# A bias network's third layer: tiles of 16 keys with two lane sums, or tiles of 32 keys with a third lane sum by transfers

## The chip, the cores and the metric

One Trainium2 chip, one core. The metric is the device time of one execution in microseconds. The kernel before was run three times: 2618.71, 2620.34 and 2621.09 us, median 2620.34. One further execution was taken by the hardware profiler.

## The reference, cut to what matters

The module has two layers: a deformable attention with an MLP behind it, and a plain attention. The change is in the first layer's attention. It has 16 groups (batch 2 times 8 heads), each with 1024 queries (32 x 32 pixels) and 64 keys at positions that the network itself has computed. For every pair of a query and a key, a small network of three layers turns the difference of their positions into one number, which is added to the product of query and key:

```python
pos = grid_q[:, :, None, :] - grid_kv[:, None, :, :]      # 2 numbers for each pair
bias = jnp.sign(pos) * jnp.log1p(jnp.abs(pos))
bias = jax.nn.relu(bias @ cpb_w1 + cpb_b1)                # 2 -> 128   (layer 1)
bias = jax.nn.relu(bias @ cpb_w2 + cpb_b2)                # 128 -> 128 (layer 2)
bias = (bias @ cpb_w3 + cpb_b3)                           # 128 -> 1   (layer 3)
sim = jnp.einsum('bhid,bhjd->bhij', qh, kh) + bias
attn = jax.nn.softmax(sim, axis=-1)
```

That is 16 x 1024 x 64, about a million pairs, and layer 2 alone is a product of 128 x 128 for each. This bias network is most of the kernel's time.

## The kernel before, in words

**Stages.** Some 35 us of head (first queries, offsets, weights); then one loop over 256 slices, from about 35 to 1892 us; then the output projection, the MLP and the second attention layer. The change touches the loop, and a little of the head that prepares weights and the order of channels.

**A slice** is four keys of one group against all 1024 queries; a group is 16 slices (NSL), and s counts the slices through. In one slice:
- `st_layer1` (L681, DVE): one custom instruction adds two tables, ta (x part) and tb (y part), and clips below at zero, into h (three buffers). It is made two slices ahead.
- `st_layer2` (L698, TensorE): 32 matmuls of 128 x 32 weights. For each z of four sets of 32 channels, four column groups of the array take the four keys, so that partition 32 q + l of the PSUM tile holds key q and lane l. Each z is evicted by ACT with its relu (L707 for z = 0 and 2 into rx; L709 for z = 1 and 3, with a scale).
- `st_sum` (L717, DVE): one scalar_tensor_tensor adds z = 0 to z = 1, another adds z = 2 to z = 3, with layer 3's weights as the scale. The first sum is in a tile called ua, uo or uc by the slice (s % 4 = 0: ua; odd: uo; 2: uc); the second is in ub. Then a DMA issued by POOL adds ub onto the first (L719). Layer 3 is now the sum over 32 lanes, with one sign for each.

**Lane sums by transfers.** The 32 lanes of a key are not summed on TensorE alone. Transfers that accumulate (issued by POOL, L736) and plain copies (issued by SP) fold the lanes and put two slices into one tile:
- `st_fold` adds odd lanes onto even lanes (64 partitions); `st_join` copies the next slice's odd lanes into the free odd lanes on SP (L743), and adds its even lanes there. A tile now has 8 keys by 16 lane sums.
- `st_fold2` and `st_join2` do the same with lanes in twos, on two slices further (32 partitions each, two of each; SP copies at L752). A tile ua now has 16 keys by 8 lane sums.

All adds go out on POOL in one fixed order, since `add` and `st_sum` chain them:

```python
        def add(out, in_):
            with tc.issue_after(added[0]):
                nc.gpsimd.dma_start(out=out, in_=in_, accum_op=ALU.add)
            added[0] = nc.cur_bb.bb.instructions[-1]
```

**Layer 3** (`st_layer3`, L784, TensorE) multiplies such tiles by a mask of signs (w3f) and accumulates into the PSUM tile sim, which also gets the product of query and key (L767, once for two groups). It is called at s % 8 = 4 for the 8 slices that began 12 slices before: two tiles, and for each of the two halves of the queries, four matmuls in the four column groups. For the last 8 slices of all, the slices that aren't folded to the end are multiplied one by one with w3u.

**What runs beside.** `softmax_steps` (tails) takes sim of a finished group in small steps, one per slice at most, on ACT, DVE and TensorE (transposes L801 and L834). `later` (bg) samples keys and makes the next chains' offsets in small steps. `load_tables` loads fb on SP one chunk of four slices ahead. The order of each engine's instructions is fixed when the program is built: a scheduler places them by priority, and `issue_after` forces some places. Iteration s means what the loop issues for s: the sums of slice s - 1, the folds and joins that are due, layer 1 of s + 2, layer 2 of s, and then layer 3.

**Buffers.** rx 3, ub 3, uo 3, uc 2, ua 4, h 3, PSUM tiles of layer 2 three. The rank and order of the channels in the head (`rank`, `order`, `arrange`) sorts them by the sign of their weight in layer 3, so that lanes which are added without a scale carry one sign.

Of the kernel before, what the change touches and what calls it, by code (L numbers as in the profile page):

```python
# [14 lines left out]
P = 128  # L15
# [4 lines left out]
J = 64  # L20
# [37 lines left out]
def conv_seq_kernel(ctx: ExitStack, tc: tile.TileContext, x, xt, kst, pst, cst, vec, wsm, outw, w1, w2, wl, wlt, brow, out):  # L58
# [24 lines left out]
    sc = cp.tile([P, 9], F32, name="sc")  # L83
    w3f = cp.tile([P, 48], F32, name="w3f")
    w3u = cp.tile([P, 60], F32, name="w3u")
# [121 lines left out]
    with tc.tile_pool(name="lp", bufs=2) as lp:  # L207
# [33 lines left out]
        nc.gpsimd.dma_start(out=cs, in_=cst)  # L241
        nc.gpsimd.dma_start(out=pz[:, 0:413], in_=pst)
        nc.gpsimd.dma_start(out=ident, in_=kst)

        def load(b, k, wq=None):
# [25 lines left out]
        po_, rn, t8, pc, dc, k8, one = (  # L271
            pw_[:, a:b] for a, b in ((0, 1), (1, 3), (3, 4), (4, 5), (5, 6), (8, 16), (128, 256))
        )
# [14 lines left out]
        def order():  # L288
            nc.vector.tensor_scalar(k8, eight, rn[:, 1:2], 8.0, ALU.is_le, ALU.mult)
            nc.vector.tensor_reduce(t8, k8, AX.X, ALU.add)  # L290
            free, bound = ([t.rearrange("p (a b l) -> p b a l", a=2, b=2)[:, i] for t in (place, crow)] for i in (0, 1))
            nc.vector.tensor_scalar(bound[0], bound[1], t8, 64.0, ALU.is_ge, ALU.mult)
            nc.vector.tensor_tensor(bound[0], bound[0], bound[1], ALU.add)
            nc.vector.tensor_scalar(free[0], free[1], t8, None, ALU.add)
            nc.vector.tensor_scalar(perm, place, pc, None, ALU.is_equal)

        def arrange():
# [16 lines left out]
            for z in (1, 3):  # L314
                nc.gpsimd.tensor_tensor(sc[:, 4 + z : 5 + z], sc[:, 4 + z : 5 + z], sc[:, z : z + 1], ALU.mult)
            nc.gpsimd.tensor_scalar(w3f[:, 16:32], mask[:, 0:16], sc[:, 8:9], None, ALU.mult)
            nc.gpsimd.tensor_scalar(w3u[:, 28:32], mask[:, 16:20], sc[:, 8:9], None, ALU.mult)

# [3 lines left out]
        def chain(ci):  # L322
# [126 lines left out]

            fe = ph.tile([P, 5, n], F32, tag="fe", name="fe")  # L450
            pos, ab, u, ln, er = (fe[0:64, i, :] for i in range(5))
            nc.vector.tensor_scalar(pos, thf[0:64, 2 * n : 3 * n], -1.0, gq[0:64], ALU.mult, ALU.add)
            if ci > 0:
# [6 lines left out]

            nc.vector.scalar_tensor_tensor(er, u, 1.0, ab, ALU.subtract, ALU.subtract)
            rc = acc.rearrange("p a k y x -> p (a k y x)")[0:64, 0:n]
            nc.vector.reciprocal(rc, u)
            nc.vector.tensor_tensor(er, er, rc, ALU.mult)
            nc.vector.tensor_scalar(pos, pos, 0.0, 2.0, ALU.is_ge, ALU.mult)
            yield
            nc.vector.tensor_tensor(ln, ln, er, ALU.subtract)
            nc.vector.scalar_tensor_tensor(ab, pos, 1.0, ln, ALU.subtract, ALU.mult)
# [9 lines left out]
        def sample(ci):  # L478
# [9 lines left out]

            sg = ph.tile([P, 5, 2, K * J], F32, tag="fe", name="sg")
            hat = sg[:, 0:4].rearrange("p a f j -> p (a f j)")[:, 0 : 4 * K * J]  # L490
# [4 lines left out]
            nc.vector.tensor_tensor(sg[:, 4], sg[:, 0], sg[:, 1], ALU.mult)  # L495
            hx = ph.tile([P, 2, K, J], F32, tag="hx", name="hx")
            hxf = hx.rearrange("p f k j -> p (f k j)")
# [4 lines left out]
            for i, (b, k) in enumerate(G):  # L502
# [13 lines left out]

                kv, uv = (ph.tile([P, J], F32, name=name) for name in ("kv", "uv"))
                rowwise, natural = "p (e i t) -> p e i t", "p (i e t) -> p e i t"
                for f in range(2):
                    r, v = slice(64 * f, 64 * f + 64), sg[:, 4, f, i * J : (i + 1) * J]  # L520
                    nc.scalar.activation(
                        uv[r].rearrange(rowwise, e=2, t=16), v[r].rearrange(natural, e=2, t=16), AF.Copy,
                        scale=col("bn1b", k)[r],
                    )
                yield
# [5 lines left out]
                for t in range(8):  # L531
                    for f in range(2):
# [3 lines left out]
                        )  # L536
                nc.scalar.activation(
                    kv.rearrange(rowwise, e=2, t=16), ps[:, 0:J].rearrange(natural, e=2, t=16), AF.Copy,
                    scale=bns[:, k : k + 1],
                )  # L540
                nc.vector.tensor_tensor(kv, kv, uv, ALU.add)
# [149 lines left out]
        def st_layer2(s):  # L691
            h1 = h1s.pop(s)
            r = []
            for z in range(4):
                ps = zp.tile([P, 2, 512], F32, name="ps2")
                for h in range(2):
                    for q in range(4):
                        nc.tensor.matmul(  # L698
                            ps[32 * q : 32 * q + 32, h, :], cw2[:, 32 * z : 32 * z + 32],
                            h1[:, 16 * h : 16 * h + 16, q, :], start=True, stop=True,  # L700
                        )
                name, bufs = (
                    ("rx", 3), (("ua", 4), ("uo", 3), ("uc", 2), ("uo", 3))[s % 4], ("rx", 3), ("ub", 3)
                )[z]
                o = lp.tile([P, 2, 512], F32, name=name, bufs=bufs)
                if z % 2 == 0:
                    nc.scalar.activation(o, ps, AF.Relu, bias=sc[:, 4 + z : 5 + z])  # L707
                else:
                    nc.scalar.activation(o, ps, AF.Relu, bias=sc[:, 4 + z : 5 + z], scale=sc[:, z : z + 1])  # L709
# [45 lines left out]


        def st_layer3(s):
            gi, i = divmod(s // 8, NSL // 8)
            b, k, f = groups[gi]
            if gi not in sims:  # L760
                sims[gi] = simp.tile([P, 512], F32, name="sim")
            if f == 0 and i == 1:

                assert state[chain_of[b, k][0]] is None
                sims[gi + 1] = simp.tile([P, 512], F32, name="sim")
                for f_, h_, o, h in QUADS:
                    nc.tensor.matmul(  # L767
                        sims[gi + o][h_, :], kz[f_, b * NCH + k, :], qa[f_, b, k, h * 512 : (h + 1) * 512],
                        start=(o == 1), stop=False,
                    )  # L770
            w = w3f[:, 16 - 16 * i : 48 - 16 * i]
            parts = [[(w, sums[s + 4 * e][1])] for e in range(2)]
            if s + 8 == NS:

                w = [w3u[:, 28 - 16 * i - 4 * o : 60 - 16 * i - 4 * o] for o in range(4)]
                parts[1] = [(w[o], sums[s + 4 + o][1]) for o in range(4)]
                parts[1].append((w[3], sums[s + 7][3]))
                parts[0] = 4 * [None] + parts[0]
            for m in range(len(parts[1])):
                for h in range(2):  # L780
                    for e in range(2):
                        if parts[e][m]:
                            q, (w_, t) = 64 * h + 32 * e, parts[e][m]
                            nc.tensor.matmul(  # L784
                                sims[gi][q : q + 32, :], w_, t[:, h, :], start=(i == 0 and f == 0),
                                stop=(i == 1 and m == len(parts[e]) - 1),
                            )
            for o in range(8):
                sums.pop(s + o)
# [57 lines left out]
        for s in range(NS):  # L847
# [602 lines left out]
def _order(np):  # L1450
# [3 lines left out]

    place = np.where(z % 2 == 1, 8 * (l // 4) + l % 4 + 4 * (z // 2), 32 * (z // 2) + l)
    crow = np.broadcast_to(place, (P, P))
    tri = d[:, None] < d[None, :]
    eight = np.broadcast_to(8 * np.arange(1, 9), (P, 8))
    four = (4 * (d % 4) + d // 32)[:, None] == np.arange(16)
    alone = (d // 32)[:, None] == np.arange(4)  # L1460
    return np.concatenate([crow, tri, eight, d[:, None], four, alone], axis=1).astype(np.float32)

# [87 lines left out]
```

## Time and profile before

| what | value |
|---|---|
| median of 3 runs | 2620.34 us |
| profiled execution | 2621.32 us, span 2619.2 us |
| TensorE clock granted | 1.00 |
| busy in the span: PE, DVE, ACT, POOL | 2603.2, 2313.1, 1750.3, 815.7 us |
| layer 2 on TensorE (L698) | 16384 records, 1776.0 us busy |
| layer 3 on TensorE (L784, w3f) | 252 records, 35.0 us busy |
| DMA over the span | 407.74 MB, mean 156 GB/s |

How to read it: the span runs from the first to the last instruction; the execution's own time is 2.1 us longer. A line Lnnn is the line of the kernel's source. The names of tiles are printed without numbers (h1 is h, ps2 is ps, cw2 is cw). One fp32 matmul leaves two records. "Idle before" is the time that the engine stood before an instruction of the group, and the name behind the arrow is what ended it. POOL's and SP's rows are issues: the transfer itself lands some us later.

### The profile page before, as it was taken

To read this page: it belongs to the slowest core of one execution; us is meant where nothing else is said; L and a number is where in the kernel's file an instruction comes from. 1 tells how busy PE (TensorE), PEld (TensorE's weight loads), DVE (VectorE), ACT (ScalarE), POOL (GpSimd) and SP (SyncE) were. 2 spreads that over 40 slices of the span, in tenths; PEclk is the share of its full clock that TensorE was granted. 3 is DMA by queue.
4 is the path that set the end of the run, shared out by engine and by line. 5 is a ranking of instruction groups with operands and counts; after the bars stand their busy time and mean duration, and the time that the engine had idled before them with its cause. 6 is when DMAs were issued, how large, how long until landed. Compare 5 with 4: busy or idle time off the path is not lost.

```text
span 2619.2 us, 48156 instructions
## 1 busy us (share of the span) xinstructions
PE 2603.2 (99%) x19752; PEld 1019.5 (39%) x19752; DVE 2313.1 (88%) x1463; ACT 1750.3 (67%) x2325; POOL 815.7 (31%) x909
## 2 busy tenths in 40 slices
PE   9999999999999999999999999999999999999999
PEld 3333322333233232333333333334355665646556
DVE  7999999999999999999999999999776587666656
ACT  5887898878888887887887777777733242314041
POOL 1333333333333333333333333333332334200100
PEclk9999999999999999999999999999999999999999
DMA  5788877888887888787887888788787768400202
GB/s 188 176 174 185 190 171 168 182 182 195 169 178 171 180 171 200 173 179 166 185 182 165 180 177 177 167 185 177 151 211 169 150 143 172 91 17 1 73 0 57
DMA packets 167531, 407.74 MB, mean 156 GB/s; under 512 B 24944, under 2 KB 73216, under 8 KB 164624
## 3 DMA queue, kind: packets, MB, share of 16 engines
q0 software_dynamic: 100736, 259.43, 54.6%
q1 hardware_dynamic: 66144, 144.93, 15.8%
q8 instruction: 156, 2.56, 0.4%
q14 instruction: 63, 0.52, 0.1%
q10 hardware_dynamic: 432, 0.31, 0.0%
HBM read 82.15 MB, written 6.55 MB: 34 GB/s over the span
## 4 chain that ended last, share of the span: by engine, by line
PE 93%; DVE 3%; ACT 2%; issue 1%; DMA 0%; DVEq 0%; ACTq 0%
PE ps L698 64%; PE sw L1041 7%; PE sw L1200 7%; PE sw L160 6%; PE sw L988 2%; PE sw L1298 2%; PE sim L784 1%; PE psg L600 1%; DVE hm L137 1%; ACT rx L707 1%; PE psx L1276 1%; PE pkv L534 0%; PE sim L767 0%; PE pt L801 0%; PE pb L834 0%
## 5 line engine op out<-in xcount | busy, mean ns | idle before, releaser
L698 PE MATMUL ps<-h,cw 128*32 128x512 f32 x16384 | 1776.0, 592 | 6.1 <-ACT rx L707 5.0
L681 DVE CUSTOM_DVE_ANT_1 h<-ta,tb 128x4096 f32<-128x4096 f32 (+1 forms) x257 | 1130.5, 4399 | 29.6 <-PE ps L698 26.8
L698 PEld LDWEIGHTS ps<-h,cw 128*32 128x32 f32 x16384 | 538.0, 110 | 1209.1 <-issue 1144.6
L707 ACT ACTIVATE rx<-ps,sc 128x1024 f32<-128x1024 f32 x512 | 568.2, 1110 | 146.3 <-PE ps L698 125.7
L709 ACT ACTIVATE ub<-ps,sc 128x1024 f32<-128x1024 f32 x256 | 308.3, 1204 | 92.7 <-PE ps L698 92.6
L717 DVE SCALAR_TENSOR_TENSOR ub<-rx,sc,ub 128x1024 f32<-128x1024 f32 x256 | 326.3, 1275 | 6.6 <-ACT ub L709 6.6
L736 POOL DMA_DIRECT2D ua<-uc x126 | 154.8, 1241 | 301.6 <-DMA ua<-uc 291.7
L736 POOL DMA_DIRECT2D ua<-ua x189 | 219.0, 1319 | 28.8 <-DMA ua<-uo 22.3
L719 POOL DMA_DIRECT2D uo<-ub x127 | 124.4, 980 | 232.3 <-DVE ub L717 217.6
L1041 PE MATMUL sw<-hm,w2t 128*128 128x512 f32 x448 | 193.8, 592 | 0.2 <-DVE hm L125 0.2
L709 ACT ACTIVATE uo<-ps,sc 128x1024 f32<-128x1024 f32 x128 | 154.3, 1205 | 51.4 <-PE ps L698 51.0
L717 DVE SCALAR_TENSOR_TENSOR uo<-rx,sc,uo 128x1024 f32<-128x1024 f32 x128 | 163.3, 1276 | 8.1 <-ACT uo L709 8.1
L736 POOL DMA_DIRECT2D uc<-uo x63 | 53.1, 842 | 319.4 <-DMA uc<-uo 314.4
L1041 PEld LDWEIGHTS sw<-hm,w2t 128*128 128x128 f32 x448 | 85.0, 190 | 104.3 <-issue 99.0
L137 DVE TENSOR_TENSOR hm<-hm,sw 128x512 f32<-128x512 f32 (+1 forms) x80 | 58.7, 738 | 70.4 <-PE sw L160 50.6
L719 POOL DMA_DIRECT2D ua<-ub x64 | 58.9, 921 | 170.8 <-DVE ub L717 163.5
L661 ACT ACTIVATE ta<-fb,vs 128x512 f32<-128x512 f32 (+1 forms) x65 | 89.3, 1377 | 8.0 <-DMA fb<-fdr 8.0
L709 ACT ACTIVATE ua<-ps,sc 128x1024 f32<-128x1024 f32 x64 | 77.1, 1204 | 20.4 <-PE ps L698 20.1
L709 ACT ACTIVATE uc<-ps,sc 128x1024 f32<-128x1024 f32 x64 | 77.2, 1206 | 20.2 <-PE ps L698 17.1
L1364 POOL DMA_DIRECT2D xs<-rs x6 | 7.2, 1195 | 259.2 <-DVE rs L137 259.2
L166 ACT COPY hm<-sw 128x512 f32<-128x512 f32 x24 | 14.1, 586 | 110.1 <-PE sw L160 110.1
L717 DVE SCALAR_TENSOR_TENSOR uc<-rx,sc,uc 128x1024 f32<-128x1024 f32 x64 | 81.6, 1275 | 2.7 <-ACT uc L709 2.5
(294 smaller groups left out, 2657.7 us busy)
## 6 DMA issues: line engine op xcount, KB each, us to landing
uo<-ub POOLq DMA_DIRECT2D x127, 512.0 KB, 5.5
fb<-fdr SPq DMA_DIRECT2D x64, 512.0 KB, 5.2
ua<-ub POOLq DMA_DIRECT2D x64, 512.0 KB, 5.7
uc<-ub POOLq DMA_DIRECT2D x64, 512.0 KB, 5.1
ua<-ua POOLq DMA_DIRECT2D x63, 256.0 KB, 6.2
ua<-uo SPq DMA_DIRECT2D x63, 256.0 KB, 2.4
ua<-uo POOLq DMA_DIRECT2D x63, 256.0 KB, 5.8
uc<-uc POOLq DMA_DIRECT2D x63, 256.0 KB, 6.9
```

What stands on the lines that cost most here:

```text
L137: nc.vector.tensor_tensor(out, a, b_, op)
L160: nc.tensor.matmul(bank[:, e, :], w, x, start=(q in (1, 2, 5) and e == k == 0), stop=True, skip_group_check=True,)
L661: nc.scalar.activation(ta.rearrange("p j x -> p x j")[:, :, j0:j1], fb[:, 0, :, j0:j1], AF.Identity, bias=col("cb1"), scale=col("w1x"),)
L681: nc.vector._custom_dve(TENSOR_ADD_SAT, out=h1[:, y : y + step].rearrange("p y t x -> p (y t x)"), in0=a.unsqueeze(1).to_broadcast([P, ste ...
L698: nc.tensor.matmul(ps[32 * q : 32 * q + 32, h, :], cw2[:, 32 * z : 32 * z + 32], h1[:, 16 * h : 16 * h + 16, q, :], start=True, stop=True,)
L707: nc.scalar.activation(o, ps, AF.Relu, bias=sc[:, 4 + z : 5 + z])
L709: nc.scalar.activation(o, ps, AF.Relu, bias=sc[:, 4 + z : 5 + z], scale=sc[:, z : z + 1])
L717: nc.vector.scalar_tensor_tensor(r[1], r[0], sc[:, z : z + 1], r[1], ALU.mult, ALU.add)
L719: nc.gpsimd.dma_start(out=sums[s][1], in_=sums[s][3], accum_op=ALU.add)
L736: nc.gpsimd.dma_start(out=out, in_=in_, accum_op=ALU.add)
L1041: nc.tensor.matmul(ps[:, m, :], w[:, a, k, m * P : (m + 1) * P], x[:, b_, k, :], start=(k == 0), stop=(k == 1),)
L1200: nc.tensor.matmul(ps[:, m, :], w[:, a, k, c + m * P : c + (m + 1) * P], x[b_][:, k, :], start=(k == 0), stop=(k == nk - 1),)
```

## The change

Tiles of 16 keys become tiles of 32 keys. After fold2 and join2, a third pair sums lanes in fours: `st_fold3` adds half of the remaining lanes onto the other half (four adds of 16 partitions on POOL), `st_join3` copies four slices' further lanes into the free ones (four copies of 16 partitions on SP), and `st_give3` adds the other half there (four adds on POOL, one iteration later than the copies). A tile now has 32 keys by 4 lane sums. `st_layer3` is called once for a group (16 slices), at s % 16 = 6, for the slices that began 22 before; it issues the product of query and key for both groups of a pair at f = 0. The four ua buffers become three u8 and two u4. Keys stay in natural order, which removes the reordering views in `sample`. The scaled channels get one sign over all 64 of them instead of in blocks of eight. To make room, some sampling tiles share buffers.

```diff
-        w2t, crow, tri, eight, chan, mask = (
-            pz[:, a:b] for a, b in ((0, 128), (128, 256), (256, 384), (384, 392), (392, 393), (393, 413))
+        w2t, crow, tri, chan, mask = (
+            pz[:, a:b] for a, b in ((0, 128), (128, 256), (256, 384), (384, 385), (385, 437))
         )
...
         def order():
-            nc.vector.tensor_scalar(k8, eight, rn[:, 1:2], 8.0, ALU.is_le, ALU.mult)
-            nc.vector.tensor_reduce(t8, k8, AX.X, ALU.add)
+            nc.vector.tensor_scalar(t8, rn[:, 1:2], 64.0, 64.0, ALU.is_ge, ALU.mult)
...
-            hx = ph.tile([P, 2, K, J], F32, tag="hx", name="hx")
+            hx = ph.tile([P, 2, K, J], F32, tag="acc", name="hx")
...
-                kv, uv = (ph.tile([P, J], F32, name=name) for name in ("kv", "uv"))
+                both = ph.tile([P, 2, J], F32, tag="gof", name="both")
+                kv, uv = both[:, 0], both[:, 1]
...
                 name, bufs = (
-                    ("rx", 3), (("ua", 4), ("uo", 3), ("uc", 2), ("uo", 3))[s % 4], ("rx", 3), ("ub", 3)
+                    ("rx", 3), (("u8", 3), ("uo", 3), ("uc", 2), ("uo", 3), ("u4", 2), ("uo", 3), ("uc", 2), ("uo", 3))[s % 8],
+                    ("rx", 3), ("ub", 3),
                 )[z]
...
+        def fours(s, i):
+            t = sums[s][1].rearrange("(l a e) h n -> l a e (h n)", a=2, e=4)[:, i]
+            return [t[:, e] for e in range(4)]
+
+        def st_fold3(s):
+            for o, i in zip(fours(s, 0), fours(s, 1)):
+                add(o, i)
+
+        def st_join3(s):
+            for o, i in zip(fours(s, 1), fours(s + 4, 1)):
+                nc.sync.dma_start(out=o, in_=i)
+
+        def st_give3(s):
+            for o, i in zip(fours(s, 1), fours(s + 4, 0)):
+                add(o, i)
...
         def st_layer3(s):
-            gi, i = divmod(s // 8, NSL // 8)
+            gi = s // NSL
             b, k, f = groups[gi]
-            if gi not in sims:
-                sims[gi] = simp.tile([P, 512], F32, name="sim")
-            if f == 0 and i == 1:
+            if f == 0:
                 assert state[chain_of[b, k][0]] is None
-                sims[gi + 1] = simp.tile([P, 512], F32, name="sim")
+                for o in range(2):
+                    sims[gi + o] = simp.tile([P, 512], F32, name="sim")
...
-            w = w3f[:, 16 - 16 * i : 48 - 16 * i]
-            parts = [[(w, sums[s + 4 * e][1])] for e in range(2)]
-            if s + 8 == NS:
-                w = [w3u[:, 28 - 16 * i - 4 * o : 60 - 16 * i - 4 * o] for o in range(4)]
-                parts[1] = [(w[o], sums[s + 4 + o][1]) for o in range(4)]
-                parts[1].append((w[3], sums[s + 7][3]))
-                parts[0] = 4 * [None] + parts[0]
+            w = w3f[:, 0:32]
+            parts = [[(w, sums[s + 8 * i][1])] for i in range(2)]
+            if s + NSL == NS:
+                w = [w3u[:, 12 - 4 * o : 44 - 4 * o] for o in range(4)]
+                parts[1] = [(w3f[:, 32:64], sums[s + 8][1])] + [(w[o], sums[s + 12 + o][1]) for o in range(4)]
+                parts[1].append((w[3], sums[s + 15][3]))
+                parts[0] = 5 * [None] + parts[0]
...
+            if s % 8 == 0 and s >= 8:
+                st_fold3(s - 8)
+            if s % 8 == 4 and s >= 12:
+                st_join3(s - 12)
+            if s % 8 == 5 and s >= 13:
+                st_give3(s - 13)
...
-            if s % 8 == 4 and s >= 12:
-                st_layer3(s - 12)
-                if s % NSL == 4:
-                    tails.append(softmax_steps(s // NSL - 1))
+            if s % NSL == 6 and s > NSL:
+                st_layer3(s - 22)
+                tails.append(softmax_steps(s // NSL - 1))
         st_sum(NS - 1, 2)
-        st_layer3(NS - 8)
+        st_layer3(NS - NSL)
```

More of the change, by code (lines that the diff above doesn't have):

```diff
@@ L83, in conv_seq_kernel @@
     sc = cp.tile([P, 9], F32, name="sc")
-    w3f = cp.tile([P, 48], F32, name="w3f")
+    w3f = cp.tile([P, 64], F32, name="w3f")
     w3u = cp.tile([P, 60], F32, name="w3u")
@@ L241, in conv_seq_kernel @@
         nc.gpsimd.dma_start(out=cs, in_=cst)
-        nc.gpsimd.dma_start(out=pz[:, 0:413], in_=pst)
+        nc.gpsimd.dma_start(out=pz[:, 0:437], in_=pst)
         nc.gpsimd.dma_start(out=ident, in_=kst)
@@ L259, in conv_seq_kernel @@
         uo = vp[:, NCH : 2 * NCH, :]
-        w2t, crow, tri, eight, chan, mask = (
-            pz[:, a:b] for a, b in ((0, 128), (128, 256), (256, 384), (384, 392), (392, 393), (393, 413))
+        w2t, crow, tri, chan, mask = (
+            pz[:, a:b] for a, b in ((0, 128), (128, 256), (256, 384), (384, 385), (385, 437))
         )
         wb = vs[:, VOFF["w3"] : VOFF["w3"] + 2]
-        po_, rn, t8, pc, dc, k8, one = (
-            pw_[:, a:b] for a, b in ((0, 1), (1, 3), (3, 4), (4, 5), (5, 6), (8, 16), (128, 256))
+        po_, rn, t8, pc, dc, one = (
+            pw_[:, a:b] for a, b in ((0, 1), (1, 3), (3, 4), (4, 5), (5, 6), (128, 256))
         )
@@ L315, in arrange @@
                 nc.gpsimd.tensor_tensor(sc[:, 4 + z : 5 + z], sc[:, 4 + z : 5 + z], sc[:, z : z + 1], ALU.mult)
-            nc.gpsimd.tensor_scalar(w3f[:, 16:32], mask[:, 0:16], sc[:, 8:9], None, ALU.mult)
-            nc.gpsimd.tensor_scalar(w3u[:, 28:32], mask[:, 16:20], sc[:, 8:9], None, ALU.mult)
+            nc.gpsimd.tensor_scalar(w3f[:, 0:48], mask[:, 0:48], sc[:, 8:9], None, ALU.mult)
+            nc.gpsimd.tensor_scalar(w3u[:, 28:32], mask[:, 48:52], sc[:, 8:9], None, ALU.mult)
         state = {}
@@ L448, in chain @@
             place_keys(2 if ci == 0 else 0, 3)
-            fe = ph.tile([P, 5, n], F32, tag="fe", name="fe")
-            pos, ab, u, ln, er = (fe[0:64, i, :] for i in range(5))
-            nc.vector.tensor_scalar(pos, thf[0:64, 2 * n : 3 * n], -1.0, gq[0:64], ALU.mult, ALU.add)
+            fe = ph.tile([P, 3, n], F32, tag="fe", name="fe")
+            ab, u, ln = (fe[0:64, i, :] for i in range(3))
+            pos = thf[0:64, 2 * n : 3 * n]
+            nc.vector.tensor_scalar(pos, pos, -1.0, gq[0:64], ALU.mult, ALU.add)
             if ci > 0:
@@ L486, in sample @@
                 yield
-            sg = ph.tile([P, 5, 2, K * J], F32, tag="fe", name="sg")
-            hat = sg[:, 0:4].rearrange("p a f j -> p (a f j)")[:, 0 : 4 * K * J]
+            sg = ph.tile([P, 3, 2, K * J], F32, tag="fe", name="sg")
+            hat = sg[:, 0:2].rearrange("p a f j -> p (a f j)")
             nc.scalar.activation(hat, gx, AF.Abs, bias=edge[:, 0:1])
@@ L536, in sample @@
                         )
[L537 to L540, printed above, removed]
+                nc.scalar.activation(kv, ps[:, 0:J], AF.Copy, scale=bns[:, k : k + 1])
                 nc.vector.tensor_tensor(kv, kv, uv, ALU.add)
@@ L768, in st_layer3 @@
                         sims[gi + o][h_, :], kz[f_, b * NCH + k, :], qa[f_, b, k, h * 512 : (h + 1) * 512],
-                        start=(o == 1), stop=False,
+                        start=True, stop=False,
                     )
-            w = w3f[:, 16 - 16 * i : 48 - 16 * i]
-            parts = [[(w, sums[s + 4 * e][1])] for e in range(2)]
-            if s + 8 == NS:
-                w = [w3u[:, 28 - 16 * i - 4 * o : 60 - 16 * i - 4 * o] for o in range(4)]
-                parts[1] = [(w[o], sums[s + 4 + o][1]) for o in range(4)]
-                parts[1].append((w[3], sums[s + 7][3]))
-                parts[0] = 4 * [None] + parts[0]
+            w = w3f[:, 0:32]
[5 more added lines that the diff above has]
+                parts[0] = 5 * [None] + parts[0]
             for m in range(len(parts[1])):
                 for h in range(2):
-                    for e in range(2):
-                        if parts[e][m]:
-                            q, (w_, t) = 64 * h + 32 * e, parts[e][m]
+                    for i in range(2):
+                        if parts[i][m]:
+                            q, (w_, t) = 64 * h + 32 * i, parts[i][m]
                             nc.tensor.matmul(
-                                sims[gi][q : q + 32, :], w_, t[:, h, :], start=(i == 0 and f == 0),
-                                stop=(i == 1 and m == len(parts[e]) - 1),
+                                sims[gi][q : q + 32, :], w_, t[:, h, :], start=False,
+                                stop=(m == len(parts[i]) - 1),
                             )
-            for o in range(8):
+            for o in range(NSL):
                 sums.pop(s + o)
@@ L1453, in _order @@
     z, l = d // 32, d % 32
-    place = np.where(z % 2 == 1, 8 * (l // 4) + l % 4 + 4 * (z // 2), 32 * (z // 2) + l)
+    place = 32 * (z // 2) + l
     crow = np.broadcast_to(place, (P, P))
     tri = d[:, None] < d[None, :]
-    eight = np.broadcast_to(8 * np.arange(1, 9), (P, 8))
+    eight = (4 * (d % 8) + d // 32)[:, None] == np.arange(32)
     four = (4 * (d % 4) + d // 32)[:, None] == np.arange(16)
     alone = (d // 32)[:, None] == np.arange(4)
-    return np.concatenate([crow, tri, eight, d[:, None], four, alone], axis=1).astype(np.float32)
+    return np.concatenate([crow, tri, d[:, None], eight, four, alone], axis=1).astype(np.float32)
 def _layout(np, inputs):
```

16 lines of the change are left out of this document (6 added, 10 removed).

## The prediction, made before the changed kernel was run

> **What bounds the kernel now.** I read the page first (busy shares, then the chain that ended last), then the loop alone (60 to 1890 us) as one stretch, then the groups of TensorE, then who waited for whom, and last the timelines of TensorE and POOL around one place where layer 3 stands.
>
> From the page, busy shares and the chain:
>
> ```profile
> PE 2603.2 (99%) x19752; PEld 1019.5 (39%) x19752; DVE 2313.1 (88%) x1463; ACT 1750.3 (67%) x2325; POOL 815.7 (31%) x909
> PE 93%; DVE 3%; ACT 2%; issue 1%; DMA 0%; DVEq 0%; ACTq 0%
> ```
>
> The loop as one stretch (length, busy time of PE, PEld, DVE, ACT, POOL, clock, DMA share, GB/s), and TensorE's groups:
>
> ```profile
> 60.00:1890.00 1830.00, 1824.67 (x17064) 570.23 (x17060) 1783.06 (x898) 1495.06 (x1936) 650.19 (x758) 1.00 0.82 177
> ...
> L698 PE MATMUL ps<-h,cw 128*32 128x512 f32 x16384 | 1776.0, 592 | 6.1 <-ACT rx L707 5.0 <-ACT ub L709 0.7
> ...
> L784 PE MATMUL sim<-ua,w3f 128*32 128x512 f32 x252 | 35.0, 596 | 0.0
> ```
>
> TensorE sets the loop: it is idle 5 us of 1830, and DVE 47 us. The clock is 1.00 throughout, so it explains nothing here. Each matmul has two records. L784, layer 3, has 0.0 us of idle time before it: its inputs, which come through four kinds of transfers, are there when TensorE reaches it. That is what the change puts at risk, so the question is how early they are.
>
> Who waited in the loop, for DVE, and for POOL in the whole run (total us, times, longest):
>
> ```profile
> DVE h L681 <- PE ps L698: 26.8, 36, 0.9
> ...
> POOL uc L736 <- DMA uc<-uo: 314.4, 61, 9.4
> POOL ua L736 <- DMA ua<-uc: 291.7, 55, 7.7
> ...
> POOL uo L719 <- DVE ub L717: 217.6, 76, 10.2
> POOL ua L719 <- DVE ub L717: 163.5, 54, 10.2
> ```
>
> POOL is busy only 31%, but it issues in order and stands hundreds of us in waits for landings. Its free time is what it waits for DVE: 217.6 + 163.5 us, and 29.7 us for uc (same view), 411 us in all.
>
> Now the place itself, in group 14. The pair L767, L784 follows slice 20 of a group with f = 0. TensorE, then POOL:
>
> ```profile
> 1811.87 1.09 PE L767 MATMUL sim<-qa,kz 64*64 64x512 f32 x8
> 1812.88 1.06 PE L784 MATMUL sim<-ua,w3f 128*32 128x512 f32 x8
> 1813.77 20.78 PE L698 MATMUL ps<-h,cw 128*32 128x512 f32 x192
> ```
>
> ```profile
> 1818.93 1.19 POOL L719 DMA_DIRECT2D ua<-ub  x1
> 1827.92 0.84 POOL L736 DMA_DIRECT2D uc<-uo  x1 [7.80 <-DMA uc<-uo]
> 1828.46 1.21 POOL L719 DMA_DIRECT2D uo<-ub  x1
> 1829.03 1.50 POOL L736 DMA_DIRECT2D ua<-ua  x1
> 1829.56 1.82 POOL L736 DMA_DIRECT2D ua<-uc  x1
> ```
>
> 192 records take 20.7 us, 0.108 each, so the two slices 21 and 22 (128 records) end at 1813.77 + 13.8 = 1827.6. The add uc<-uo, the one that opens iteration 21 on POOL after the sum ua<-ub, waited 7.80 us for its SP copy and went out at 1827.92, later than the end of slice 22. POOL's issues follow each other by 0.53 to 0.57 us.
>
> **What it removes.** Of 31 regular layer-3 sets (four matmuls in four column groups) 15 stay. A set costs 1813.77 - 1812.88 = 0.89 us in this place and 0.86 in others; at 0.87, 16 sets are 13.9 us. The last set gets one more pass of two matmuls, which costs 0.86 us (in the old last set such passes start at 1892.05 and 1892.91). Sum: -13.0 us, all on TensorE, the engine that sets the loop.
>
> **What it adds on POOL and SP.** For each of 31 pairs of tiles: four adds (st_fold3), four copies on SP, four adds (st_give3): 248 POOL issues at 0.55 us, 136 us, covered by the 411 us that POOL waits for DVE; without that cover they would cost up to 136 us. The four folds go out behind the fold of the twos, where the next instruction waits for DVE by 3 us; the four copies stand on SP ahead of the table load fb, whose data are needed 20 us later. Neither is on the path. Each new transfer is 64 KB beside 3.5 MB of POOL's adds in four slices, 7% more. [...]
>
> **The wait that it adds.** Layer 3 of a group now stands on TensorE after slice 22, and needs the last four adds (st_give3 of its second tile). In the instruction order of the built program these stand on POOL directly behind that uc<-uo of iteration 21, and the second layer-3 matmul waits for them. In group 14 they would go out at 1828.5, 1829.0, 1829.6 and 1830.1 and land L later. TensorE comes earlier than before: the old pair L767, L784 (1811.87 to 1813.77, 1.9 us) no longer stands ahead of slice 21, so slice 22 ends at 1825.7, L767 runs to 1826.7, and TensorE stands until 1830.1 + L.
>
> L has no row for 16 partitions. From the DMA issues of the loop:
>
> ```profile
> uc<-uo POOLq DMA_DIRECT2D x63, 256.0 KB, 3.3
> ua<-uc POOLq DMA_DIRECT2D x126, 128.0 KB, 5.6
> ```
>
> Its ends are 2.5 us (the last ua<-uc of the loop, alone in its queue, issued at 1888.27, landed at 1890.81) and 6.8 us (ua<-ua of 128 KB, queued behind others). I take 3.3, because uc<-uo is what these adds are issued next to, into the same drained queue.
>
> The same two views for all 15 groups give uc<-uo minus the end of slice 22: from -3.8 us (group 2) to +2.7 (group 7), mean -0.7. The wait per group is then -0.7 + 0.87 (the layer-3 set gone ahead of slice 21; where L767 moves too, it is run after) + 2.2 (four issues) + 3.3 = 5.7 us. One thing shortens it: while TensorE stands, POOL catches up. In iteration 19 it issues its sum 2.8 us after DVE has it; if it were never late, the chain would come some 2.5 us sooner. The new issues pull the other way; I take 0.9 off: 4.8 us, times 15 = 72 us. The ends are 2.4 us (L = 2.5, POOL never late; 36 us) and 9.2 us (L = 6.8; 138 us).
>
> Behind that wait on TensorE stand the 32 matmuls of slice 23; ACT waits for them, DVE fills its three h buffers and stops. Nothing of it runs on to make the time good: TensorE was the engine without idle time. What it does give back is TensorE's own small waits, the 5.0 us for ACT.
>
> **Other edits.** The sampling buffers share tags (hx with acc, kv and uv with gof); each is written long after its last reader in the same order of stages, so 0 us, with an upper end of 5 us (eight heads, one 0.6 us copy waited for) and a lower of -1 us for the one DVE reduction that the ordering loses. The softmax steps start two slices later and run in the slots they had: 0.
>
> **Sum**, against the profiled execution's own 2621.3 us (span 2619.2): 2621.3 - 13.0 + 72 - 5 = 2675.3. That execution was 1.0 above the median of 2620.3, so I say 2674.
>
> **Rivals.**
> - Faster (7%). The adds land before TensorE comes: the mechanism is POOL's chain running at least 6 us earlier than in the old trace. For it: in five groups (2, 4, 8, 10, 11) uc<-uo already precedes the end of slice 22 by 2.4 to 3.8 us. Against it: the chain fold, copy, add is made of landings, not of POOL's speed. It decides where the mean wait falls under 0.9 us. Then -13.0 is left, of which DVE gives back up to 5 us, since half of the groups leave it without idle time: 2609 to 2613, say 2611.
> - No change (3%): a wait of about 0.9 to 1.2 us a group eats just what is saved; 2615 to 2625.
> - POOL becomes the bound (5%). If each of the 31 periods pays two more landings of 6.8 us in order, 422 us, its 1419 us of work and waits for transfers become 1841, above the loop's 1830; ub comes free late, ACT and then TensorE stop. With the waits at layer 3 that gives some 2740 to 2770. Against it: the new folds and copies find their inputs landed.
> - My forecast (85%): slower by the wait at layer 3, 2639 to 2714 (2714 is L = 5.1, the landing of uc<-ub, with POOL as late as now).
>
> The range is 2636 to 2714: it leaves out the first two rivals, the third, and the far end of L. A difference of 0.2%, 5.2 us, is about what a measurement can tell; beyond it: faster 0.07, within 0.03, slower 0.90.
>
> **What would show it.** In the changed profile, layer 3 must have idle time before it that ends on a DMA of the new tiles, 15 times, some 5 us each, and TensorE's busy time in the loop must fall by 13 us while the loop grows by some 55. The second layer-3 matmul should start within half a us of a give3 landing. ACT's and DVE's waits for PE must grow by about as much. If layer 3 again shows no idle time, the step that puts the four adds behind uc<-uo, or L, is wrong; if POOL's waits for DVE vanish, the third rival holds; if idle time sits on ub or rx instead, it is buffers.

## The result, and the profile after

| kernel | median, us | runs | ratio to before, 95% interval |
|---|---|---|---|
| before | 2619.58 | 4 | |
| changed | 2773.57 (2770.89 to 2775.30) | 4 | 1.0586 (1.0568 to 1.0605) |

The change costs 154 us where 54 were forecast, and the time lies above the range (2636 to 2714). The sign and the place were right; the size was not.

The page of the changed kernel, busy shares and the chain that ended last:

```profile
PE 2643.7 (95%) x19628; PEld 1055.4 (38%) x19628; DVE 2315.9 (83%) x1462; ACT 1748.9 (63%) x2325; POOL 1008.6 (36%) x1157
PE 44%; DMA 35%; DVE 9%; issue 8%; POOL 3%; ACT 0%; POOLq 0%; SPq 0%; DVEq 0%
```

That chain was 93% PE before; now a third of it is DMA. TensorE stands idle 130 us of the span (16 before), and is also busy 40 us longer although it has less to do. TensorE's groups show both:

```profile
L692 PE MATMUL ps<-h,cw 128*32 128x512 f32 x16384 | 1824.4, 599 | 13.7 <-ACT rx L702 12.7 <-ACT ub L704 0.7
...
L795 PE MATMUL sim<-u,w3f 128*32 128x512 f32 x128 | 45.9, 878 | 105.2 <-DMA u<-u 104.8 <-issue 0.4
```

L795 is layer 3 (L784 before, where idle was 0.0): 104.8 us of waits for a give3 landing, 15 of them, 2.1 to 10.2 us long. But its records also last 878 ns instead of 596, and layer 2 (L692) is 48 us busier for the same 16384 records, some of them beside layer 3's longer ones. The stretches around one of these waits (length, then busy time of PE, PEld, DVE, ACT, POOL, clock, DMA share, GB/s) say why:

```profile
718.40:725.30 6.90, 3.92 (x30) 0.73 (x22) 6.90 (x5) 4.18 (x10) 1.09 (x3) 1.00 0.50 127
725.40:735.60 10.20, 5.16 (x27) 1.89 (x31) 0.61 (x1) 0.00 (x0) 7.12 (x9) 0.50 0.97 179
735.60:742.40 6.80, 6.80 (x68) 2.79 (x64) 2.72 (x2) 4.87 (x5) 0.84 (x1) 1.00 0.51 117
```

The granted clock is 0.50 for 10.2 us, part of it after the wait. There are 15 such spells before the end of the loop: one behind each wait at layer 3 but the shortest (2.1 us), and one behind a wait of 8.8 us for ACT. Together they are 119 us, in which TensorE is busy 66, so 33 us of work is lost. The prediction had no such term.

The same place on TensorE, then on POOL:

```profile
720.25 1.09 PE L778 MATMUL sim<-qa,kz 64*64 64x512 f32 x8
721.27 1.05 PE L795 MATMUL sim<-u,w3f 128*32 128x512 f32 x2
730.44 1.08 PE L795 MATMUL sim<-u,w3f 128*32 128x512 f32 x3 [8.12 <-DMA u<-u]
```

```profile
713.40 1.68 POOL L714 DMA_DIRECT2D u<-ub  x1
724.21 0.84 POOL L731 DMA_DIRECT2D uc<-uo  x1 [9.13 <-DMA uc<-uo]
724.75 3.40 POOL L731 DMA_DIRECT2D u<-u  x4
726.73 2.34 POOL L714 DMA_DIRECT2D uo<-ub  x1
```

This is the picture that was forecast: the four adds of `st_give3` (u<-u x4) go out directly behind uc<-uo, which waits 9.13 us for its copy, and layer 3 resumes when they land, at 730.44. Only the times are later. Slice 22 ended at 719.8 (the start of its last record plus 0.108, as the prediction counts), so uc<-uo came 4.4 us behind it. The last line matters too: the next sum, uo<-ub, was held up behind all five.

Against a kernel without the new transfers, whose layer 3 stands one slice later (noxfer below, span 2610.1), the changed one is 163 us longer. TensorE is idle 112 us more: 103 at layer 3, and 9 where it waited for ACT and ACT for a load of in_x (below). It is busy 51 us more: 33 at half clock, and 18 that I put down to layer 3's matmuls, which are started in two parts around the wait and no longer run beside each other (at full clock, two records take 1.05 us at 721.27, where eight took 1.06 in the old place). L795 is busy 45.9 us against 19.0, 25 of it at half clock; in unblock22 (below), where the clock is down for 10 us in all, it is still 33.6.

### The profile page after: what moved, and what is told of

Same layout as the page of the kernel before. It is cut to its first block, busy times and chain, and to the rows that moved or that the text cites. A ratio compares the mean times of both kernels' runs of the same rounds, so it can differ in the third digit from the quotient of the medians.

```text
span 2773.5 us, 48768 instructions
## 1 busy us (share of the span) xinstructions
PE 2643.7 (95%) x19628; PEld 1055.4 (38%) x19628; DVE 2315.9 (83%) x1462; ACT 1748.9 (63%) x2325; POOL 1008.6 (36%) x1157
## 4 chain that ended last, share of the span: by engine, by line
PE 44%; DMA 35%; DVE 9%; issue 8%; POOL 3%; ACT 0%; POOLq 0%; SPq 0%; DVEq 0%
PE ps L692 19%; DMA uc<-uc 10%; DMA uc<-uo 9%; PE sw L1057 7%; PE sw L160 6%; PE sw L1216 6%; DMA u<-u 5%; DMA u<-uc 4%; DMA uc<-ub 3%; DVE h L675 3%; DMA u<-uo 3%; PE sw L1004 2%; PE sw L1314 2%; DVE ub L712 1%; POOL u L731 1%
## 5 line engine op out<-in xcount | busy, mean ns | idle before, releaser
L692 PE MATMUL ps<-h,cw 128*32 128x512 f32 x16384 | 1824.4, 599 | 13.7 <-ACT rx L702 12.7
L692 PEld LDWEIGHTS ps<-h,cw 128*32 128x32 f32 x16384 | 577.9, 111 | 1214.0 <-issue 1146.8
L731 POOL DMA_DIRECT2D u<-u x437 | 434.4, 1633 | 43.7 <-DMA u<-uo 25.4
L731 POOL DMA_DIRECT2D u<-uc x126 | 183.9, 1473 | 198.0 <-DMA u<-uc 189.3
L714 POOL DMA_DIRECT2D uo<-ub x127 | 170.7, 1344 | 163.2 <-DVE ub L712 124.5
L795 PE MATMUL sim<-u,w3f 128*32 128x512 f32 x128 | 45.9, 878 | 105.2 <-DMA u<-u 104.8
L731 POOL DMA_DIRECT2D u<-uo x63 | 60.4, 958 | 226.5 <-DMA u<-uo 223.3
L714 POOL DMA_DIRECT2D u<-ub x64 | 75.0, 1171 | 80.8 <-DVE ub L712 70.5
L704 ACT ACTIVATE u<-ps,sc 128x1024 f32<-128x1024 f32 x64 | 77.1, 1205 | 20.7 <-PE ps L692 20.3
```

The source lines that it names most:

```text
L692: nc.tensor.matmul(ps[32 * q : 32 * q + 32, h, :], cw2[:, 32 * z : 32 * z + 32], h1[:, 16 * h : 16 * h + 16, q, :], start=True, stop=True,)
L714: nc.gpsimd.dma_start(out=sums[s][1], in_=sums[s][3], accum_op=ALU.add)
```

## The experiments

The comparisons with an interval rest on 4 to 11 runs; the others on one run each, good to some 0.2%.

### Layer 3 later (later1, later2b)

```diff
-            if s % NSL == 6 and s > NSL:
-                st_layer3(s - 22)
+            if s % NSL == 7 and s > NSL:      # later2b: == 8, s - 24
+                st_layer3(s - 23)
```

> Layer 3 of a group stands one slice later on TensorE (after slice 23 instead of 22), all else as in the changed kernel. Theory A (TensorE waits at layer 3 for the last four third-layer adds, and its clock halves because of that wait): the one slice, 6.9 us, fills most of each wait. Of the 15 waits of the changed kernel (2.1 to 10.2 us, 104.8 in all) what exceeds 6.9 us is left, 15 us in all; the 119 us at half clock, which cost 60, all but vanish. 2773.5 - 105 + 15 - 60 = 2624 us, between 2612 and 2645. Theory B (the loop is short of transfers or of POOL's time, and the wait at layer 3 is only where it shows): the wait turns up elsewhere, in front of evictions into ub, and the time stays over 2700 us.

> Layer 3 stands two slices later (after slice 24). It then holds the first of the three buffers of its tiles while slice 24 wants it, so ACT's eviction of that slice waits a few us each group. Theory A: no wait for a landing is left at layer 3 (the longest was 10.2 us, two slices are 13.8), the clock stays at 1.00; 2773.5 - 105 - 60 = 2609 us and 15 times 0 to 2 us for the buffer, 2609 to 2640. If the buffer costs more than one slice's wait did, this kernel is slower than the one with layer 3 a single slice later. Theory B (short of transfers): over 2700 us.

Measured: later1 2687.21 us, ratio 1.0260 (1.0243 to 1.0277); later2b 2698.31, 1.0305 (1.0290 to 1.0321). Neither time lies in a range that was given, and both theories hold in part. Moving layer 3 gives back 86 of 154 us, but not the 150 that theory A asked for. In later1 36.9 us of waits are left at layer 3. In later2b 11.4 are left, and something else has come up, which the waits of POOL inside the loop and those of ACT show:

```profile
POOL uc L731 <- DMA uc<-uo: 408.4, 59, 11.2
POOL u L731 <- DMA u<-uo: 242.5, 69, 8.8
POOL u L731 <- DMA u<-uc: 197.4, 38, 8.0
POOL uc L731 <- DMA uc<-ub: 61.2, 29, 3.6
POOL uo L714 <- DVE ub L712: 32.8, 8, 10.2
```

```profile
ACT ub L704 <- DMA uo<-ub: 59.5, 32, 5.8
...
ACT ub L704 <- DMA uc<-ub: 49.7, 24, 4.6
...
ACT ub L704 <- DMA u<-ub: 43.5, 19, 4.1
```

POOL stands 927 us in waits for landings and only 63 in waits for DVE; its sums go out 5.1 to 8.1 us after DVE has them, in the means of the three kinds (0.4 to 2.5 before), ub comes free late, and ACT waits 153 us for it. That is the third rival of the prediction, by its own test: POOL's waits for DVE vanish, and ACT and then TensorE stop. The chain was there all along; in the changed kernel the stop at layer 3 seems to have hidden it, since POOL catches up while TensorE stands (there its sums go out 1.3 to 3.2 us after DVE). Waits of POOL in the loop up to 1890 us, for landings and for DVE: before 728 and 425, changed 807 and 229, later1 898 and 93.

### The clock by itself (busy40, busy20)

```diff
+            dm = flat("dm")
+            for o in range(40):               # busy20: 20
+                q = 32 * (o % 4)
+                nc.tensor.matmul(dm[q : q + 32, 0:512], cw2[:, 0:32], qa[:, b, k, 0:512], start=True, stop=True)
```

> Layer 3 stays after slice 22, but TensorE first does 40 matmuls of no use (128x32 on 128x512, 0.216 us each, 8.6 us) in front of it in 15 groups, so that it stands idle little while it waits. Theory A with the clock as a cost of its own: the wait is still paid, as work, but the clock stays at 1.00: 2773.5 less half of 119 us, 60, and some 10 us more where the wait was shorter than 8.6 us: 2724 us, 2712 to 2740. If the halved clock costs nothing beside the wait itself: 2773 + 10, some 2784 us.

> The changed kernel (layer 3 after slice 22) with 20 matmuls of no use in front of layer 3, 4.3 us, so that they fit inside nearly every wait. Wait and filling together should come to the 105 to 115 us that the wait has alone; the clock should fall only where more than some 2.2 us of idle time is left in one window of 3.4 us: 30 to 50 us at half clock instead of 119. Clock as a cost of its own: 2773.5 - 35 + 0 to 10 = 2733 to 2752 us. Clock without cost: 2770 to 2785 us.

Measured: 2770.60 and 2768.23 us, 3 and 5 us less than the changed kernel, which one run each hardly tells from nothing. In busy40 the time at half clock falls from 119 to 7 us and layer 2 from 1824 to 1785 us busy, so some 30 us of work come back; but the matmuls of no use and the rest of the wait come to 146 us instead of 105. Two things account for most of what is lost again: uc<-uo stands 4.4 us behind the end of slice 22 in the mean (3.4 in the changed kernel), 16 us in 15 groups, and in 4 groups the filling runs past the landing, 10 us. So a TensorE that runs faster between two waits met POOL's adds later, and the terms do not simply add. busy20 gives back less to begin with: half clock falls to 51 us, which is 12 us of work and not the 35 that I had forecast, and filling and wait are 118; uc<-uo is no later there (3.4). What the clock costs by itself is not shown by either run.

### What makes POOL late: the number of adds, their bytes, or their order (nofold3, halfbytes, unblock1)

nofold3 is the changed kernel without the four adds of st_fold3; halfbytes is later1 with every third-layer transfer cut to half its columns:

```diff
-            if s % 8 == 0 and s >= 8:
-                st_fold3(s - 8)
```

```diff
-            return [t[:, e] for e in range(4)]
+            return [t[:, e, 0:512] for e in range(4)]
```

> The four adds of the third layer's first half (st_fold3) are left out, so half of the third sums is missing; copies, the last adds and layer 3 stay where they are. It tests why POOL comes 4 us later to the last adds than in the kernel before. Theory A1 (the added transfers queue ahead of the sums and of the copies): POOL's add uc<-uo moves from 3.4 us behind the end of slice 22 to 0.7 to 2, the wait at layer 3 falls from 105 us to 65 to 85, the time at half clock from 119 to some 70: 2710 to 2745 us. A2 (it is only that slice 22 ends earlier, or how the adds happen to fall): 2765 to 2780 us.

> later1 with each third-layer transfer cut to half its columns (32 KB instead of 64 KB; half of the third sums is missing); as many issues, as many waits. Theory D (bytes): half of what later1 lies above 2606 us goes, 2640 to 2652 us. Theory C (order and latency of the chain on POOL): little changes, 2675 to 2690 us.

unblock1 is later1 with every transfer kept and POOL's order alone changed. An add that waits for a copy of SP goes behind the next slice's sum:

```diff
         def st_join(s):
             nc.sync.dma_start(out=lanes(s, 1), in_=lanes(s + 1, 1))
+        def st_give(s):
             add(lanes(s, 1), lanes(s + 1, 0))
...
+            if s % 2 == 0 and s >= 4:
+                st_give(s - 4)
...
-            if s % 4 == 0 and s >= 4:
-                st_fold2(s - 4)
+            if s % 4 == 1 and s >= 5:
+                st_fold2(s - 5)
...
+            if s % 4 == 3 and s >= 7 and s < NS - 1:
+                st_give2(s - 7)               # the adds of st_join2, one iteration later
...
-            if s % 8 == 0 and s >= 8:
-                st_fold3(s - 8)
+            if s % 8 == 1 and s >= 9:
+                st_fold3(s - 9)
```

> Layer 3 after slice 23, as in later1, and POOL's instruction order changed: every add that waits for a copy of SP (st_join's, st_join2's) now stands behind the next slice's sum, where its copy should have landed, and fold2 and fold3 stand one slice later. All transfers stay. It tests what is left of later1 (2687 us). Theory C (POOL's order: it stands in front of adds whose copies are still under way, so each sum behind goes out late, and the new adds and copies lengthened that chain beyond the period): POOL's waits for landings fall from over 900 us to under 500, the sums go out at once, no wait over 2 us is left at layer 3, clock 1.00: 2619 - 13 + up to 15 = 2606 to 2625 us. Theory D (bytes or transfers: the DMA engines, 0.87 busy in later1, are the limit whatever the order): 2670 to 2700 us.

Measured: nofold3 2777.50, no change (theory A2), with 111.9 us of waits at layer 3 and uc<-uo 3.6 us behind the end of slice 22. So the 124 issues that it leaves out are not it; which of the others are is not shown one by one. halfbytes 2656.33, 31 us less than later1, with uc<-uo 3.1 us behind the end of slice 22 instead of 4.8: how long the chain's transfers take counts, more than theory C allowed (2656 lies near the range of theory D). unblock1 2625.88, ratio 1.0026 (1.0017 to 1.0035): 61 us less than later1 with the same transfers. POOL's waits inside the loop, unblock1:

```profile
POOL u L714 <- DVE ub L712: 249.0, 62, 7.9
POOL uc L714 <- DVE ub L712: 197.6, 55, 7.8
POOL u L731 <- DMA u<-uc: 187.5, 50, 8.4
POOL uo L714 <- DVE ub L712: 172.7, 80, 10.2
POOL uc L731 <- DMA uc<-uo: 84.5, 38, 7.3
```

Waits for landings fall from 898 to 303 us, those for DVE rise from 93 to 657: POOL again has its free time. The add uc<-uo, which stood 9.13 us in the lines of the changed kernel, now finds its copy landed or nearly so:

```profile
678.17 0.85 POOL L714 DMA_DIRECT2D u<-ub  x1 [3.91 <-DVE ub L712]
678.71 5.11 POOL L731 DMA_DIRECT2D u<-u  x6
685.03 0.89 POOL L714 DMA_DIRECT2D uo<-ub  x1 [1.21 <-DVE ub L712]
688.14 0.84 POOL L731 DMA_DIRECT2D uc<-uo  x1 [2.22 <-DMA uc<-uo]
```

So theory C holds in the main, and D falls: the DMA engines are 0.90 busy in unblock1 (0.87 in later1), and the loop is faster. unblock1 moves the adds of both joins and both later folds at once; what each is worth was not measured.

### The saving alone, and the order in the old place (noxfer, unblock22, ub_before)

noxfer is later1 without st_fold3, st_join3 and st_give3; unblock22 is the changed kernel with unblock1's order and layer 3 still after slice 22; ub_before is the kernel before with that order.

> later1 without any transfer of the third layer (fold3, join3, give3 left out, so the third sums are missing); layer 3 still does 15 sets and reads the same tiles, and the sampling buffers stay as changed. It measures the saving alone and the edits costed at nothing. If they cost nothing: 2619 - 13 = 2606, up to 5 us given back by VectorE: 2603 to 2613 us. If the sampling buffers or the split tiles cost something of their own: 2615 to 2640 us.

> The changed kernel with POOL's order alone changed as in unblock1; layer 3 stays after slice 22. In unblock1 the last adds of a group go out 17.4 to 18.9 us after the start of slice 20 and land 6.6 us later, 4.9 us behind the end of slice 22. So TensorE would still wait 3.5 to 4.6 us a group, some 60 us, and the clock would halve in part of the windows (10 to 20 us lost), with the one late load of unblock1 on top: 2606 + 17 + 60 + 15 = 2698, 2670 to 2710 us. If the place of layer 3 were all that mattered, 2760 to 2775 us as in the changed kernel; if POOL's order were all, 2620 to 2630.

> The kernel before (two layers of sums, layer 3 in its old places) with POOL's order changed in the same way, nothing else. TensorE bounds it and has no idle time to give, so the order should bring nothing: 2616 to 2622 us. If layer 3, which stands where the old order just delivered, now waits for adds that go out later: 2625 to 2680 us.

Measured: noxfer 2611.61, ratio 0.9968 (0.9956 to 0.9981), so the saving, with all other edits, is 8 us. unblock22 2660.52: in the very place that the prediction spoke of, POOL's order alone is worth 113 of the 154 us; 17 us of waits are left at layer 3, fewer than the 60 I had expected:

```profile
L799 PE MATMUL sim<-u,w3f 128*32 128x512 f32 x128 | 33.6, 603 | 17.3 <-DMA u<-u 15.2 <-DMA u<-uc 2.1
```

The add uc<-uo is as late there as in the changed kernel (3.8 us behind the end of slice 22, 3.4 there). But the four adds of `st_give3` no longer stand behind it: the first goes out 4.1 us ahead of that end instead of 3.9 us behind it, and the last lands 4.0 us behind it instead of 9.4.

ub_before 2660.24, 1.0156 (1.0142 to 1.0170): there the new order sends the last adds out later than the old place of layer 3 allows; layer 3 stands 18.7 us in waits and is busy 54.0 us instead of 35.0. Order and place belong together. The order by itself does not explain why a kernel with three layers could win.

### What is left of unblock1 (win1, two_steps, act_load, act_rings)

Group by group, from the first matmul of one to that of the next, unblock1 agrees with noxfer within 0.1 us in 14 of 15, and differs in one, 129.2 against 116.1 us. There ACT waits for a load of in_x:

```profile
329.11 1.24 ACT L329 ACTIVATE xn<-xn,vs,bns 128x1024 f32<-128x1024 f32 x1 [12.97 <-DMA xn<-in_x]
```

The load went out on SP at 315.9 us and landed 13.2 us later. What it overwrites is free when the four matmuls that read it are done on TensorE, at 307.9 us (the expectations name copies on ACT, which end at 310.7; but before, the load went out at 307.55, ahead of those copies). In between, SP issued two copies of the third layer (310.6 to 314.4 us) and a table load. It is the same load that costs 9 us in the changed kernel. All four runs start from unblock1: win1 and two_steps give the side work (`later`) idle steps, in win1 behind the wrong load; act_load lets ACT issue the load; act_rings moves the table loads to ACT as well and has one idle step.

```diff
-            nc.sync.dma_start(out=xn, in_=xv[:, k, b, :])
+            on = nc.scalar if (b, k) not in [c[0] for c in CHAINS] else nc.sync
+            on.dma_start(out=xn, in_=xv[:, k, b, :])
...
```

> unblock1 (layer 3 after slice 23, POOL's adds behind the next sum) with two idle steps of the side work behind the one load of in_x that ACT waited 13 us for. The wait of 11.4 us on TensorE and the 10.2 us at half clock behind it should go: 2625.9 - 11.4 - 5.1 = 2609 us, 2605 to 2614, which is faster than the kernel before by 0.2 to 0.6%. If another load comes late instead: 2620 to 2630 us.

> unblock1 with two idle steps of the side work behind the load of in_x that came late there (win1 had put them behind the wrong load, one chain of heads earlier, which moved all later loads). unblock1 differs from noxfer by one group alone, 129.2 against 116.1 us. If that load is all that is left and the third layer's transfers then cost nothing: 2626 - 13 = 2613, 2609 to 2616 us, faster than before by 0.1 to 0.4%. If moved steps bring other loads late, as in win1: 2620 to 2645 us.

> unblock1 with the loads of in_x and wq inside a chain of heads issued by ACT instead of SP; the side work keeps its steps. In unblock1 the late load went out on SP at 315.9 us, 5.7 us behind the copy on ACT that frees its buffer, and took 13.2 us. If SP's order and its ring are the cause: it goes out 5 us earlier, lands in 5 to 8 us, and 7 to 12 us of the 13 go: 2613 to 2620 us. If the DMA engines are simply full there: 2623 to 2630 us.

> act_load with the table loads fb on ACT as well, and one idle step of the side work behind the late load. SP then has the copies of the sums alone. No wait for a load should be left: 2609 to 2614 us. If ACT, which now issues 64 loads more, waits in front of them: 2615 to 2630 us.

Measured: win1 2640.61, ratio 1.0075 (1.0062 to 1.0089), with ACT now 26.7 us in waits for table loads (7.8 in unblock1); two_steps 2631.95, 1.0052 (1.0039 to 1.0065), 17.7 us of the same; act_rings 2627.13, 1.0035 (1.0021 to 1.0049), with ACT in two new waits for landings, 7.7 and 5.3 us. Shifting the side work made other loads come late. act_load 2613.50, 0.9978 (0.9970 to 0.9987): the load goes out at 306.0 and lands at 312.3, before ACT needs it. That kernel is 0.2% faster than the kernel before. Its loop as one stretch, and its layer 3:

```profile
60.00:1890.00 1830.00, 1823.40 (x16982) 564.95 (x16976) 1784.34 (x901) 1499.13 (x1950) 842.25 (x1006) 1.00 0.91 191
```

```profile
L800 PE MATMUL sim<-u,w3f 128*32 128x512 f32 x128 | 19.8, 599 | 1.5 <-DMA u<-uc 1.4 <-DMA u<-u 0.2
```

TensorE is as full as it was before, the clock is 1.00, and all the transfers of the third layer lie beside it. noxfer is 2 to 3 us faster; as it has neither POOL's new order nor the load on ACT, that is only about what the transfers still cost.

## Why the prediction was right or wrong, point by point

The sum was 100 us too low. The wait at layer 3 was 33 us longer than its term. Three costs had no term at all: 33 us of work at half clock, some 18 that go with layer 3 in two parts, 9 for a load of in_x. And of the saving with what TensorE should give back, 18 us, half came.

- **The wait at layer 3 (+72 us): right mechanism, wrong size, 105 us.** Of its terms the landing L = 3.3 us was near (the last of the four adds takes 4.0 in most groups), and so were the four issues. Wrong was the place of uc<-uo: I took it from the old trace, -0.7 us to the end of slice 22, and let 0.9 more off for POOL catching up. Measured in the changed kernel: +3.4 us in the mean, where noxfer, without the new transfers, has +1.0: so the larger part came with them. Some of that was made good by 2.4 us a group that TensorE still worked between the end of slice 22 and the wait, most of which the sum left out. The chain in front of it had lengthened step by step (means over 15 groups, before and after): the sum ub onto uo goes out 0.4 and 1.6 us after DVE, lands in 7.6 and 9.1, SP's copy goes out 1.5 and 1.8 later and lands in 4.0 and 4.5 us. I had timed the new adds in a trace that did not hold them.
- **"248 POOL issues at 0.55 us, 136 us, covered by the 411 us that POOL waits for DVE": this step failed.** A sum over the loop is no cover. POOL's free time lies at its waits for DVE; the new adds and copies lengthen the waits for landings in between (728 us before, 807 in the changed kernel, 898 in later1), in order, and every sum behind pays. nofold3 shows that half of the new adds can go without any gain, unblock1 and unblock22 that the order decides.
- **"The clock is 1.00 throughout, so it explains nothing here": true of the old kernel and a trap for the new one.** The waits on TensorE had a follow-up cost of their own, 33 us at half clock and some 18 for layer 3 in two parts. I priced the stand and not what comes after. That this cost would come off by itself if the clock were kept up is not shown (busy40, busy20).
- **The copies on SP, costed at nothing.** In unblock1, which has them too, one load of the heads went out late behind them on SP and stopped TensorE 11 us; in the changed kernel the same load stopped it 9. I had looked at the table loads fb, which have room; the load of in_x had none: before, ACT started on it in the moment it landed, at 316.5 us.
- **The saving (-13.0) and the other edits (0): 8 us together**, by noxfer, in which TensorE is 10.6 us less busy and 1.5 us more idle than before. The two were not measured apart. The forecast for the case without waits, 2609 to 2613 with up to 5 us given back, was right (2611.6).
- **The third rival (5%, 2740 to 2770)** had the mechanism that lies beneath: POOL's in-order waits. Its test was stated rightly, and later2b meets it. Its price, 2740 to 2770, was for it together with the waits at layer 3; later2b, almost without those waits, takes 2698. It should not have been a rival to the wait at layer 3, since POOL's lateness is what makes that wait long. At 5% it was far too small.

The size of a single transfer did not tell what the third layer's transfers cost. Halved to 32 KB, POOL's new adds land in 4.1 us instead of 4.7 (medians in the loop, halfbytes and later1); but halving them took 31 us off later1, and placed well all of them cost about 2 us. In the changed kernel the 248 adds of 64 KB took 4.9 us in the median, and 3.0 at least.

## What to carry to other kernels

Free time of an engine that issues in order is worth something only where it lies: before adding work, list its waits one by one, and see which ready instruction stands behind each that is not. An issue that waits for another queue's transfer belongs behind the next thing that is ready anyway; here that alone turned 61 us. And when a change makes TensorE wait where it never did, take the inputs' time from a chain that already holds the new work, and add what the clock does after the wait (here 33 us of work).

## What the runs showed of the hardware that I had not expected

In the trace of the changed kernel the 15 spells at half clock are recorded at 0.50 for 3.413, 6.827 or 10.240 us, and all start on one grid of 3.413 us, from the first at 210 us to the last at 1971. With the records of TensorE from 60 to 2050 us laid on that grid, at full clock each of the 15 windows that were busy 0.37 or less was followed by one at 0.50, and none of the 533 that were busy 0.43 or more. In the traces of ten other runs of this case the windows part between 0.40 and 0.44 as well; only in nofold3 do they not, with a window at 0.43 that was followed by half clock and one at 0.41 that was not. The fullest of the 15 windows stood idle for 2.2 us. How a wait fell on the grid counted too: in busy20 one of 2.9 us inside a window was followed by half clock, and one of 3.1 us across two was not. One drop came when the wait was already over (at 1107.7 us, 1.0 us after it).

Filling the waits to keep that clock up brought only 3 to 5 us (busy40, busy20). And a share of 0.91 of the DMA engines' time in the loop, the highest of all these runs, belongs to act_load, the fastest kernel with all the transfers of the third layer (2613.50 us): it was no limit there.
